# A two-layer decoder on one core: the shared expert's products made to give way and wait for the last routing, and the grouped attention's norm taken per half block

## The chip, the cores and the metric

One Trainium2 chip, one core. The metric is the device time of one execution in microseconds (us). The kernel is written by hand, with one queue of instructions per engine: TensorE (PE, its weight loads PEld), VectorE (DVE), ScalarE (ACT), GpSimd (POOL) and SyncE (SP), which issues most DMAs. Each engine takes its instructions strictly in order.

## What is computed

The input `x` is 64 sequences of 64 tokens with 256 features (4096 tokens), all in float32. Two layers follow each other, each with three sublayers on a layer norm of `x`, whose results are added to `x`:

```python
x = x + _L0_attn_ref(_layernorm(x), ...)    # state-space scan (SSD)
x = x + _L0_xattn_ref(_layernorm(x), ctx)   # latent cross attention
x = x + _L0_ffn_ref(_layernorm(x), ...)     # 7 routed experts (top 2) + 1 shared expert
x = x + _L1_attn_ref(_layernorm(x), ...)    # WKV recurrence
x = x + _L1_xattn_ref(_layernorm(x), ctx, ctx)  # grouped attention, 32 query and 8 key heads
x = x + _L1_ffn_ref(_layernorm(x), ...)     # top 8 of 64, mixed in 8 groups
```

Two of them matter here. In the feed-forward of layer 0 every token goes through a shared expert (up, gate with SiLU, down: three 256x256 products) and through two of seven routed experts of the same form; which two is decided by a small product, a top-2 and a softmax. In the cross attention of layer 1 the normalised `x` is the query, scaled per token by `1/sqrt(var)` and shifted by the mean.

## The kernel before

**Units.** A tile is 128 tokens (32 of them), a half block 2 tiles (16), a block 4 tiles (8). `x` stays in SBUF for the whole run.

**Stages.** `layer0` (L1682) runs the scan and the latent attention of all half blocks and `moe_front` of the blocks 0 to 6. `moe_phase` (L1087) then runs `moe_front` of block 7, `moe_tables` and 38 expert tiles (`moe_tile`, L993). `layer1` (L1664) runs all of layer 1.

**What sets the order.** Each piece of work is a Python generator, called a stream. At build time `Plan` keeps a rough model of when each engine is free and each tile is written. `Plan.play` (L204) always continues the stream that by this model could begin first (`Plan.begin`, L197; ties go by rank), and issues its next piece, up to the next `yield`. A `yield` can name marks that other streams must have set, a number of free PSUM banks, or `ROOM`, which puts the stream in the last rank (1000 and above). What the planner issues is then the fixed order of every engine's queue; the chip does not reorder it.

**The last routing.** `moe_front` (L792) normalises one block, transposes it (`hT_ps`, `mr_hT`), writes it to DRAM (`moe_hT`, from which the shared expert reads), multiplies it with the router's weights (`lT_ps`), transposes the logits (`pl`), and picks two experts per token on DVE (`mr_gate` to `moe_oh`). A product `rk` counts the tokens ahead of each one, DVE works out the slots, and POOL scatters the rows to their experts' slots with 8 indirect DMAs (`moe_hs`). `moe_tables` (L905) then counts the rows of each expert (`cnt`) and works out on DVE which expert each of the 38 tiles belongs to (`mt_int`). SP reads that table before it can load the first tile (`ht`), which PE then transposes (`ht_ps`).

**The shared expert.** `shared(n)` (L1069) does half block n of 16. It loads `sh_hT` (two buffers), and makes three groups of four 128x256 products, `u_ps`, `g_ps` and `d_ps`, with ACT and DVE steps between them (`expert`, L1032), and adds to `x`. Each of these products is asked for with `ROOM`. The half blocks 0 to 7 are also fillers of `moe_phase`: they may begin at once, and one that has not begun when the first expert tile has is left for `layer1`, which runs all that are in `shared_left`.

**Layer 1.** Per half block: `collect` (L1649) adds the experts' rows to `x` with indirect DMAs on POOL, after the shared expert's half block; `wkv_front` and `wkv_scan` (L1145, L1205) end in `wk_po`; two streams `gqa_tile` (L1336) do the grouped attention of one tile each; then comes the feed-forward: `ffn_front` (L1456) for a group of 2 or 4 tiles, `ffn_half`, `ffn_gate` and `ffn_down` (products `gu_ps` and `acc`). The first `ffn_front` also waits for every half block in `shared_left`.

**A tile of the grouped attention.** `gqa_tile` waits for the keys, for the scan of its half block, for the tile two before it and for the feed-forward of the tile nine before it. It takes the norm of its one tile (`norm`, L287: statistics and two small steps on DVE, a power on POOL), writes the query in groups with four `tensor_scalar` of 64 columns on POOL (`gqa_q`), transposes it (`pq`), and goes on to `sc`, a maximum on DVE, `pq` again, `st`, an exponential on ACT (`pT`), `pv`, a copy of `pv` to `oT` on DVE, and `po`.

All engine instructions go through one helper, so all have line L62 in the profile; they are told apart by the tiles that they write and read.

Of the kernel before, what the change touches and what calls it, by code (L numbers as in the profile page):

```python
# [66 lines left out]
class Plan:  # L67
# [5 lines left out]


    ROOM, SOON, LAST = "room", "soon", 1000
    COST = dict(vector=(100, 1.17), scalar=(250, 0.75), gpsimd=(300, 1.75), sync=(380, 0))
    AFTER = dict(tensor=250, vector=150, scalar=150, gpsimd=200, sync=100)

# [118 lines left out]
    def begin(self, item):  # L197

        at, rank, count, stream, n = item
        if n:  # L200
            at = max(at, self.banks[n - 1][0])
        return max(at, self.free.get(self.first_at.get(self.place(stream)), 0.0)), rank, count

    def play(self, streams, fillers=()):  # L204

# [34 lines left out]
class Net:  # L240
# [551 lines left out]
    def moe_front(self, wk, w, b):  # L792

        nc, te, v, gp = self.nc, self.nc.tensor, self.nc.vector, self.nc.gpsimd

        def t(n, s, bufs=1):
            return wk.tile(s, F32, tag="mr_" + n, bufs=bufs, name="mr_" + n)

        yield self.after(("route", b - 1), *(("att", n, t) for n in (2 * b, 2 * b + 1) for t in range(2)))
        f = {}  # L800
        yield from self.norm(wk, b * NT, NT, "mn", f)
        rs, nm = f["rs"], f["nm"]
        ha = w["h"][b % 2]
        for i in range(NT):
            nc.scalar.activation(ha[0][:, i, 0:D], self.x[:, b * NT + i], AF.Identity, bias=nm[:, i:i + 1], scale=rs[:, i:i + 1])
        yield
        hT = wk.tile([P, 2, TB], F32, tag="mr_hT", bufs=1, name="mr_hT")
        for c in range(2):
            yield [1]
            ps = self.mm([P, TB], "hT_ps")  # L810
            for i in range(NT):
                te.transpose(ps[:, i * P:(i + 1) * P], ha[0][:, i, c * P:(c + 1) * P], self.ident)
            yield
            (v.tensor_copy if c else nc.scalar.copy)(hT[:, c], ps)
            self.give(ps)
        yield
        self.load(self.hTd[b], hT)
        self.plan.mark("rows", b)
        nc.scalar.copy(ha[1][:, :, 0:D], ha[0][:, :, 0:D])

        yield [1]
        pq = self.mm([P, P], "lT_ps")
        for c in range(2):
            for i in range(NT):
                te.matmul(pq[32 * i:32 * i + 32], w["r"][:, c], hT[:, c, i * P:(i + 1) * P], start=c == 0, stop=c == 1)
        yield
        lT = t("lT", [P, P])
        nc.scalar.copy(lT, pq)
        self.give(pq)
        yield [1]  # L830
        pl = self.mm([P, NT, 32], "pl")
        te.transpose(pl.rearrange("p n e -> p (n e)"), lT, self.ident)
        yield
        gate, bg, eq, s1 = t("gate", [P, NT, 7]), t("bg", [P, NT, 7]), t("eq", [P, NT, 7]), t("s1", [P, NT])
        oh = w["oh"][:, b]
        v.tensor_add(gate, pl[:, :, 0:7], bc(w["br"], 1, NT))
        self.give(pl)
        v.tensor_add(bg, gate, bc(w["gb"], 1, NT))

        for k in range(2):  # L840
            v.tensor_reduce(s1, bg, AX.X, ALU.max)
            v.tensor_tensor(eq, bg, bc(s1, 2, 7), ALU.is_equal)
            v.tensor_mul(eq, eq, bc(w["rank"], 1, NT))
            v.tensor_reduce(s1, eq, AX.X, ALU.max)
            v.tensor_tensor(oh[:, k], eq, bc(s1, 2, 7), ALU.is_equal)
            if k == 0:
                v.scalar_tensor_tensor(bg, oh[:, 0], -3e38, bg, ALU.mult, ALU.add)
        yield

        both, run = t("both", [P, NT, 7]), w["run"][b % 2]  # L850
        v.tensor_add(both, oh[:, 0], oh[:, 1])
        v.tensor_copy(run[:, 0], w["total"])
        for i in range(NT):
            v.tensor_add(run[:, i + 1], run[:, i], both[:, i])
        w["total"] = run[:, NT]
        yield

        sel, g2, mx, s2 = t("sel", [P, 2, NT, 7]), t("g2", [P, 2, NT]), t("mx", [P, NT]), t("s2", [P, NT])
        v.tensor_mul(sel, oh, bc(gate, 1, 2))
        v.tensor_reduce(g2, sel, AX.X, ALU.add)  # L860
        v.tensor_tensor(mx, g2[:, 0], g2[:, 1], ALU.max)
        v.tensor_sub(g2, g2, bc(mx, 1, 2))
        yield
        nc.scalar.activation(g2, g2, AF.Exp)
        yield
        yield [1]
        rk = self.mm([P, NT, 7], "rk")
        te.matmul(rk, w["before"], both, start=True, stop=False)
        te.matmul(rk, w["ones"], run[:, 0:NT], start=False, stop=True)
        yield  # L870
        slot = t("slot", [P, NT, 7])
        v.tensor_add(slot, rk, bc(w["slot"], 1, NT))
        self.give(rk)
        v.tensor_mul(sel, oh, bc(slot, 1, 2))
        at = w["at"][:, b]
        v.tensor_reduce(at, sel, AX.X, ALU.add)
        v.tensor_copy(w["slots"][:, b], at)
        v.tensor_add(s2, g2[:, 0], g2[:, 1])
        v.reciprocal(s2, s2)
        for k in range(2):  # L880
            v.tensor_mul(ha[k][:, :, D:D + 1].rearrange("p n o -> p (n o)"), g2[:, k], s2)
        yield [("zeros", 0), ("zeros", 1)]
        for k in range(2):
            for i in range(NT):
                yield [Plan.SOON]
                self.moe_row(w, w["slots"][:, b, k, i:i + 1], ha[k][:, i])
        self.plan.mark("route", b)
# [181 lines left out]
    def shared(self, n, fills=False):  # L1069

        if fills:
            yield [Plan.ROOM] + ([("made", MAXT - 4)] if n >= 8 else [])
            if ("begun", 0) in self.plan.marks and n < 8:
                return
            self.shared_left.remove(n)
        wk = self.mid
        yield self.after(("rows", n // 2), ("shared", n - 2))
        b = wk.tile([P, 2, 2, HT], F32, tag="hT", bufs=2, name="sh_hT")
        hT, uT = b[:, 0], b[:, 1]
        self.load(hT, self.hTd[n // 2][:, :, (n % 2) * HT:(n % 2 + 1) * HT])  # L1080
        yield [Plan.ROOM, 1]
        ps = yield from self.expert(wk, None, hT, 4, True, *self.shared_mats, uT, "aT")
        self.nc.vector.tensor_add(self.x[:, 2 * n:2 * n + 2], self.x[:, 2 * n:2 * n + 2], ps)
        self.give(ps)
        self.plan.mark("shared", n)
# [238 lines left out]
    def gqa_turned(self, wk, qa, tag):  # L1324
# [8 lines left out]
        yield [4]  # L1333
        return qT

    def gqa_tile(self, wk, w, n, f):  # L1336
        nc, te, v, gp = self.nc, self.nc.tensor, self.nc.vector, self.nc.gpsimd
        t = n % NT
        yield self.after(("keys", n // NT), ("scan", n // 2), ("gqa", n - 2), ("ffn", n - GQA_LEAD))
        r_ = {}  # L1340
        yield from self.norm(wk, n, 1, "gn", r_)
        qa = w["q"][n % len(w["q"])]
        gp.memset(qa.rearrange("p g k c -> p (g k) c")[:, :, 16:18], 0.0)
        xg = self.x[:, n].rearrange("p (k j g d) -> p g k j d", k=4, j=2, g=4)
        for g in range(4):
            gp.tensor_scalar(qa[:, g, :, 0:16].rearrange("p k (j d) -> p k j d", j=2), xg[:, g], r_["rs"], r_["nm"], ALU.mult, ALU.add)
        qT = yield from self.gqa_turned(wk, qa, "qT")

        sc = [self.mm([P, 4, 2, S], "sc") for _ in range(4)]
# [26 lines left out]
                          start=True, stop=True)  # L1376
        yield
        oT = wk.tile([P, 4, P], F32, tag="oT", bufs=2, name="oT")
        v.tensor_copy(oT, pv.rearrange("p g j s -> p g (j s)"))
        self.give(pv)  # L1380
        yield [1]
        po = self.mm([P, 4, 8, 16], "po")
# [281 lines left out]
    def layer1(self, wk, w_wkv, w_gqa, w_ffn):  # L1664
        self.wkv_padded(wk, w_wkv)
        streams = [(0, self.shared(n)) for n in self.shared_left] + [(1, x) for x in [self.load_ffn(w_ffn), self.prep_ffn(wk, w_ffn)]]
        fs = [{} for _ in range(NH + NBLK)]
        streams += [(n, self.collect(n)) for n in range(NH)]
        for n in range(NH):
            streams += [(n, self.wkv_front(wk, w_wkv, n, fs[n])), (n, self.wkv_scan(wk, w_wkv, n, fs[n]))]  # L1670
        for b in range(NBLK):
            g = fs[NH + b]
            streams.append((2 * b, self.gqa_front(wk, w_gqa, b, g)))
            streams += [(2 * b + t // 2, self.gqa_tile(wk, w_gqa, NT * b + t, g)) for t in range(NT)]
        for i, (n0, nt) in enumerate(self.GROUPS):
            f = {}
            streams.append((n0 // 2, self.ffn_front(wk, w_ffn, i, n0, nt, f)))
            streams += [(h, self.ffn_half(wk, w_ffn, i, h, f)) for h in range(n0 // 2, (n0 + nt) // 2)]
        with self.tc.manual_schedule():
            self.plan.play(streams)  # L1680
# [113 lines left out]
```

## Time and profile before

| what | us |
|---|---|
| median of 3 runs | 2126.09 (2123.85 to 2131.75) |
| the profiled execution | 2121.44 |
| its span, from first to last instruction | 2119.7 |
| busy in the span: PE, DVE, POOL, ACT | 1933.7 (91%), 1343.7 (63%), 845.6 (40%), 791.1 (37%) |

The profiled execution lies 4.65 below the median and 1.74 above its own span. By the timeline `layer0` ends near 823, the first expert tile is transposed at 887, the last product of the expert tiles starts at 1094, the first WKV transpose (`wk_hT`) of layer 1 stands at 1118.9, and the first `gu_ps` at 1251.5. Times in what follows are from the start of the span. In lists of the timeline a line is: start, duration, engine, line, operation, tile written and tiles read, shapes, number of instructions, and in brackets the engine's idle time before it and what ended it. A float32 product of the program is two MATMUL instructions in the trace.

### The profile page before, as it was taken

The numbers are of one execution on the slowest core, as the hardware profiler recorded it, in microseconds if no ns is written. First come the engines' busy times: TensorE is split into PE (matmuls) and PEld (weight loads), VectorE is DVE, ScalarE is ACT, GpSimd is POOL, SyncE is SP. The second block draws the span as 40 slices with busy tenths as digits, with TensorE's granted clock in tenths as the row PEclk, the third lists the DMA queues.
The fourth block names the chain that finished last, engine by engine and source line by source line (L and its number), as shares of the span: only waits on it lengthen the run. The fifth ranks groups of instructions, "written<-read, shape, count | busy, mean of one in ns | idle before, by whom it ended". The sixth has DMA issues, their size and how long they took to land. (4 is left out here: it accounts for less than half of the span.)

```text
span 2119.7 us, 36371 instructions
## 1 busy us (share of the span) xinstructions
PE 1933.7 (91%) x13735; PEld 1548.6 (73%) x13735; DVE 1343.7 (63%) x3149; ACT 791.1 (37%) x1439; POOL 845.6 (40%) x1045
## 2 busy tenths in 40 slices
PE   7989898898989897899988879989899999999998
PEld 6768677687778775688876557767677777777777
DVE  5667776767676773343336887877778676755331
ACT  3425343434334332244433423433334334243220
POOL 2332434343534423111126856667456334432211
PEclk9989999999899998999998879989999999999999
DMA  7963200000000001388844212121111101010010
GB/s 206 348 202 118 67 16 22 16 22 16 22 26 26 22 31 67 132 302 281 276 159 91 29 21 35 15 35 22 22 20 24 19 14 18 9 23 15 17 23 11
DMA packets 167807, 150.43 MB, mean 71 GB/s; under 512 B 76153, under 2 KB 155408, under 8 KB 167632
## 3 DMA queue, kind: packets, MB, share of 16 engines
q1 hardware_dynamic: 152464, 121.61, 19.6%
q0 software_dynamic: 15168, 26.50, 5.1%
q8 instruction: 109, 1.79, 0.3%
q14 instruction: 66, 0.54, 0.1%
HBM read 88.01 MB, written 60.04 MB: 70 GB/s over the span
## 5 line engine op out<-in xcount | busy, mean ns | idle before, releaser
L62 PE MATMUL gu_ps<-hT,ffn_gu 128*128 128x256 f32 x1408 | 337.0, 386 | 5.0 <-DVE gqa_q L62 4.1
L62 PEld LDWEIGHTS gu_ps<-hT,ffn_gu 128*128 128x128 f32 x1408 | 260.2, 192 | 50.4 <-issue 8.4
L62 PE MATMUL acc<-ffn_d,aT 128*128 128x256 f32 x704 | 166.0, 389 | 9.2 <-DVE aT L62 9.2
L62 POOL TENSOR_TENSOR aT<-aT,ffn_sc 128x512 f32<-128x512 f32 (+1 forms) x48 | 69.1, 1440 | 229.1 <-DVE aT L62 197.1
L62 PEld LDWEIGHTS acc<-ffn_d,aT 128*128 128x128 f32 x704 | 134.4, 194 | 34.3 <-DVE aT L62 10.7
L62 PE MATMUL proj<-sf_hT,w_in 128*128 128x256 f32 x640 | 148.2, 389 | 0.0
L62 ACT ACT_TABLE_LOAD x104 | 133.4, 1283 | 21.4 <-PE st L62 7.9
L62 PEld LDWEIGHTS proj<-sf_hT,w_in 128*128 128x128 f32 x640 | 121.7, 194 | 18.5 <-issue 1.8
L62 PE MATMUL po<-xa_vo,ctxT 128*128 128x256 f32 x512 | 121.8, 394 | 4.9 <-ACT ctxT L62 2.8
L62 ACT ACTIVATE aT<-gu_ps 128x512 f32<-128x512 f32 x96 | 48.7, 559 | 203.4 <-PE gu_ps L62 203.3
L62 DVE TENSOR_TENSOR aT<-aT,gu_ps 128x512 f32<-128x512 f32 x96 | 56.9, 633 | 106.2 <-ACT aT L62 106.2
L62 PE MATMUL q_ps<-xn_hT,xa_q 128*128 128x256 f32 x512 | 118.3, 386 | 2.5 <-DVE ctxT L62 1.3
L62 PEld LDWEIGHTS po<-xa_vo,ctxT 128*128 128x128 f32 x512 | 99.4, 198 | 23.1 <-ACT ctxT L62 7.8
L62 POOL DMA_INDIRECT x_sb<-moe_ys,left x64 | 106.6, 1665 | 23.3 <-issue 12.0
L62 PEld LDWEIGHTS q_ps<-xn_hT,xa_q 128*128 128x128 f32 x512 | 96.3, 192 | 22.0 <-ACT xn_hT L62 2.7
L62 POOL DMA_DIRECT2D moe_ys<-y x38 | 26.3, 692 | 207.0 <-ACT y L62 194.4
L62 DVE TENSOR_REDUCE gqa_q<-sc 128x8 f32<-128x512 f32 x128 | 79.3, 681 | 35.4 <-PE sc L62 35.4
L62 DVE TENSOR_TENSOR x_sb<-x_sb,po 128x256 f32<-128x256 f32 x64 | 26.5, 415 | 107.5 <-PE po L62 107.4
L62 DVE SCALAR_TENSOR_TENSOR sf_acc<-proj,ssm_vec,sf_acc 128x252 f32<-128x252 f32 (+2 forms) x192 | 87.3, 472 | 7.5 <-ACT sf_acc L62 3.0
L62 POOL TENSOR_TENSOR p<-p,sm 128x1024 f32<-128x1024 f32 x32 | 60.8, 1907 | 73.0 <-DVE sm L62 42.5
L62 POOL DMA_INDIRECT moe_hs<-moe_h,moe_slots x64 | 64.4, 1006 | 56.9 <-ACT gT L62 27.1
L62 ACT COPY qT<-pq 128x512 f32<-128x512 f32 x64 | 37.4, 586 | 115.2 <-PE pq L62 115.2
(367 smaller groups left out, 4338.7 us busy)
## 6 DMA issues: line engine op xcount, KB each, us to landing
moe_hs<-moe_zero SPq DMA_DIRECT2D x30, 1088.0 KB
pack<-in_moe_pack_dram SPq DMA_DIRECT2D x38, 770.0 KB
ht<-moe_hs SPq DMA_DIRECT2D x32, 272.0 KB
moe_ys<-y POOLq DMA_DIRECT2D x32, 256.0 KB, 5.7
bias<-moe_bias SPq DMA_DIRECT2D x38, 128.0 KB
x_sb<-in_x_dram SPq DMA_DIRECT2D x8, 512.0 KB
moe_hT<-mr_hT SPq DMA_DIRECT2D x8, 512.0 KB
sh_hT<-moe_hT SPq DMA_DIRECT2D x16, 256.0 KB
```

The source lines that it names most:

```text
L62: return do(*a, **k)
```

## The change

It has five parts, all in the order of work but for two.

```diff
+    POLITE = 1500
@@ Plan.begin
-        return max(at, self.free.get(self.first_at.get(self.place(stream)), 0.0)), rank, count
+        at = max(at, self.free.get(self.first_at.get(self.place(stream)), 0.0))
+        return at + (self.POLITE if stream.__name__ == "shared" and rank >= self.LAST else 0), rank, count
@@ moe_front, behind the transpose of the logits
+        self.plan.mark("logits", b)
@@ shared
         if fills:
-            yield [Plan.ROOM] + ([("made", MAXT - 4)] if n >= 8 else [])
+            yield [Plan.ROOM, ("logits", NBLK - 1)]
@@ layer 1's attention
+    def gqa_norm(self, wk, h, f):
+
+        yield self.after(("scan", h), ("gqa", 2 * h - 3))
+        r = f["norm", h] = {}
+        yield from self.norm(wk, 2 * h, 2, "gn", r)
+        self.plan.mark("normed", h)
+
     def gqa_tile(self, wk, w, n, f):
-        yield self.after(("keys", n // NT), ("scan", n // 2), ("gqa", n - 2), ("ffn", n - GQA_LEAD))
-        r_ = {}
-        yield from self.norm(wk, n, 1, "gn", r_)
+        yield self.after(("keys", n // NT), ("normed", n // 2), ("gqa", n - 2), ("ffn", n - GQA_LEAD))
+        rs, nm = (f["norm", n // 2][k][:, n % 2:n % 2 + 1] for k in ("rs", "nm"))
-        for g in range(4):
-            gp.tensor_scalar(qa[:, g, :, 0:16].rearrange("p k (j d) -> p k j d", j=2), xg[:, g], r_["rs"], r_["nm"], ALU.mult, ALU.add)
+        for j in range(2):
+            gp.tensor_scalar(qa[:, :, :, 8 * j:8 * j + 8], xg[:, :, :, j], rs, nm, ALU.mult, ALU.add)
-        v.tensor_copy(oT, pv.rearrange("p g j s -> p g (j s)"))
+        nc.scalar.copy(oT, pv.rearrange("p g j s -> p g (j s)"))
@@ layer1
+            streams += [(h, self.gqa_norm(wk, h, g)) for h in (2 * b, 2 * b + 1)]
```

- A shared expert's product counts as 1500 ns later than it could begin when the planner picks what comes next, in `moe_phase` and in `layer1`.
- The fillers of `moe_phase` may begin only when the logits of the last block have been transposed.
- The norm of the grouped attention becomes a stream of its own, for two tiles at once.
- The query of a tile is written with two `tensor_scalar` of 128 columns instead of four of 64.
- The copy `oT` moves from DVE to ACT.

## The prediction

> **What bounds the kernel now.** First the page's busy times and slices: they say which engine to count on, and where it does not work.
>
> ```profile
> PE 1933.7 (91%) x13735; PEld 1548.6 (73%) x13735; DVE 1343.7 (63%) x3149; ACT 791.1 (37%) x1439; POOL 845.6 (40%) x1045
> ...
> PE   7989898898989897899988879989899999999998
> ...
> PEclk9989999999899998999998879989999999999999
> ```
>
> PE is the bound nearly everywhere, so work that only moves costs the same wherever PE has it. What can change is PE's idle and slow time. The slices show two holes: around slice 15, where layer 0 turns into expert tiles, and slices 20 to 23, the start of layer 1. So next the busy time of stretches whose ends I took from PE's timeline (columns: length, then busy PE, PEld, DVE, ACT, POOL with instruction counts, granted PE clock, DMA share, GB/s).
>
> ```profile
> 823.40:887.40 64.00, 50.51 (x224) 41.06 (x224) 25.72 (x91) 21.01 (x43) 13.06 (x25) 0.92 0.24 80
> 1095.60:1118.90 23.30, 13.17 (x62) 10.69 (x60) 6.49 (x17) 5.50 (x13) 10.77 (x13) 0.85 0.63 184
> 1118.90:1208.00 89.10, 76.36 (x545) 57.59 (x545) 68.51 (x119) 36.53 (x67) 71.15 (x66) 0.92 0.29 49
> 1208.00:1251.50 43.50, 31.17 (x230) 21.10 (x225) 32.61 (x64) 13.77 (x30) 23.34 (x25) 0.69 0.22 28
> 1373.00:1404.20 31.20, 19.58 (x229) 13.80 (x228) 28.64 (x66) 11.59 (x22) 19.96 (x23) 0.78 0.20 38
> 1404.20:2119.70 715.50, 684.01 (x5424) 540.85 (x5422) 432.88 (x856) 246.34 (x405) 284.25 (x327) 0.99 0.10 18
> ```
>
> From 1404 on PE is busy 684 of 715 us at clock 0.99: little to win. The other rows hold the change. Last, PE's and POOL's timeline of the first hole.
>
> ```profile
> 829.52 6.54 PE L62 MATMUL u_ps<-sh_hT,sh_w 128*128 128x256 f32 x16 [6.18 <-DMA sh_hT<-moe_hT]
> 835.90 0.60 PE L62 MATMUL hT_ps<-ident,moe_h 128*128 128x128 f32 x4
> ...
> 842.71 0.64 PE L62 MATMUL lT_ps<-mr_hT,moe_r 128*32 128x128 f32 x16
> ...
> 845.12 0.27 PE L62 MATMUL pl<-ident,mr_lT 128*128 128x128 f32 x1
> ...
> 848.68 3.62 PE L62 MATMUL g_ps<-sh_hT,sh_w 128*128 128x256 f32 x16
> 852.14 0.30 PE L62 MATMUL rk<-mr_both,moe_before 128*128 128x28 f32 x2
> ...
> 875.20 0.28 PE L62 MATMUL cnt<-moe_run,moe_ones 128*128 128x7 f32 x2
> ...
> 887.39 0.63 PE L62 MATMUL ht_ps<-ident,ht 128*128 128x128 f32 x4 [0.66 <-DMA ht<-moe_hs]
> ```
>
> The routing's short products stand in PE's queue behind the shared expert's long ones, and everything up to `ht_ps` hangs on them. `moe_h` is ready at 829.7; `hT_ps` starts at 835.9.
>
> **Part 1: the last routing, −10.** In the changed kernel's order both `hT_ps`, `lT_ps` and `pl` stand ahead of every shared product. From 829.7 I count: 8 transposes on a slow clock 2.1 (four took 1.39 after the idle time at 1118.9), two copies side by side 0.7 with hand-over 0.2, 16 `lT_ps` about 1.2, copy and `pl` 0.9: `mr_gate` near 835.1 instead of 845.9. DVE needs 3.9 from there to the end of `moe_run` (849.85), so 839.0. One `u_ps` group stands ahead of `rk`, and its load now follows the write of `moe_hT` in SP's queue: from a load's issue at 840.8 to its product at 845.2 were 4.4, an upper end. With that `rk` comes at 841, without it at 839; before, 852.1. The scatter comes as much earlier. Then the order has 10 groups of shared products between `rk` and `cnt` and 6 between `cnt` and `ht_ps` (before: 9 and 5). A group is 1.73 when PE runs on; between 852.5 and 886.7 14 groups took 34.2, so 2.44. At 2.44, 16 groups put `ht_ps` at 841 + 39 = 880, that is −7; at 1.9 at 871, −16. The chain from `cnt` to `ht_ps` (12.2) fits beside 6 groups at 2.0. I take −10, ends −5 and −16.
>
> **Part 2: what it leaves for later, +3.** Eight half blocks of the shared expert were finished in this hole; now five and two thirds are. Seven groups, 12.1 us, go behind the expert tiles. There lies cover: after its last product there (1093.77) PE waited for `x` (expert rows written, collected, normed) with 9.3 us idle ahead of `wk_hT` at 1118.9, 25.1 in all. The new order has 13 groups in that stretch where 7 were. At 2.0 each (six groups from 1095.60 to 1107.58) that is 26: cover, and 1 late. At 2.44 it is 31.7, 6.6 late. SP's loads for them are the same 16, in the same queue. I take +3; without the cover it is +12.
>
> The hole also left a slow clock: four transposes took 1.39 at 1118.9 and 0.60 at 1145.9. Likewise the first 16 `u_ps` took 6.54 after 6.18 of waiting, 3.62 later, so a cold start costs 2.9 here. Either kernel has one in part 1; part 2 loses one, which I leave as margin. The Trainium skill, "TensorE: Matmul & The Clock Gate", section "Why this matters for your kernels", speaks against part 1: it asks for no idle gaps over about 3 us between bursts, and clearing PE for the routing makes such a gap. By that rule the sum would be up to 2.9 worse, since the routing's products and the first shared ones would all run slowly; the trace agrees that PE is slow there, but it was before too, so I add nothing.
>
> **Part 3: the start of layer 1, +6.** `ffn_front` waits for the last shared half block. Before, its first transposes stood ahead of the third pair of attention tiles (1208.0, 89.1 after the first `wk_hT`). Now the last `d_ps` stands behind the fourth attention tile and `ffn_front` behind the third `wk_po` (before at 1242.5) and the fourth `wk_hT`. Against that, the first WKV products no longer wait for four shared groups between them (5 us), and with `gu_ps` not queued behind the fourth WKV its routing takes 25.6 (1208.0 to `smT_ps` 1233.6) and not 43.5. So the first `gu_ps` comes 115 + 25.6 + 8 = 149 after the first `wk_hT`, not 132.6. Work up to it, counted at the rates at which PE runs on (0.43 a 128x256 product, 0.11 a transpose, 1.08 for 8 `st`), is 97 instead of 90, so 7 of the 16 are paid in, and a few us of the rest come back in the colder stretch: +6, ends −8 and +27.
>
> **Part 4: the second stall, −12.** From 1373.0 to 1404.2 PE held some 12 us of work at those rates; it waited for a feed-forward front that came too late.
>
> ```profile
> 1377.52 4.54 PE L62 MATMUL acc<-ffn_d,aT 128*128 128x256 f32 x12 [4.08 <-DVE aT L62]
> ...
> 1388.31 1.22 PE L62 MATMUL pq<-ident,gqa_q 128*128 128x128 f32 x3 [4.04 <-POOL gqa_q L62]
> ```
>
> Between that front's transposes and the first `gu_ps` after it stood 21 us of PE work; in the new order 38, as the attention now runs ahead of the feed-forward. The front needs about 35 (1364.6 to 1400). The loss was 19. But DVE, at 28.6 of 31.2 there, has the same work to do: −12, ends −19 and 0.
>
> **Part 5: attention's norm and copies, −4.** Per tile POOL had four `gqa_q` at a median of 0.39, and 0.55 for `fr_h` of 256 columns: by interpolation 128 columns take 0.45, so 0.9 instead of 1.6. DVE loses 32 `oT` of 0.69 (22 us) and 32 small steps of 0.16; ACT gains 32 copies at 0.59 (its `qT`), beside its 37% load, and two table loads of 1.28. Waits of PE that name these are few: `pq` for POOL 11.8 in all (11 of it in single waits at 1203, 1260, 1388 and 1520; the third lies in part 4's stall), `po` for `oT` 3.9. The copy now stands behind ACT's exponentials, which its queue could make late. −4, ends −12 and +6.
>
> **Sum.** −10 + 3 + 6 − 12 − 4 = −17. The profiled execution took 2121.4, so 2104.4; it lies 4.65 below the median, to which runs will be compared: **2109**.
>
> **Rivals.** *Given back:* parts 1 and 2 cancel (−10 + 12) and parts 4 and 5 bring as little as part 3 costs: 2126 + 2 − 3 = 2125. For it: the work is the same and PE is 91% busy. Against it: the 9.3 us hole. *Slower:* the late `ffn_front`. If the first `gu_ps` comes a whole half block later (31 us, the step from the third `wk_hT` at 1186.0 to the fourth at 1217.0) with only 4 of work paid in, part 3 costs 27, and parts 4 and 5 win nothing in the same in-order queues: −10 + 3 + 27 = +20, 2146. It decides once the front costs over 7 more than it pays in. For it: PE at clock 0.69 from 1208 on, with no other work to take; against it: the faster first WKV steps. *More:* all parts near their good ends, which the 47 us of idle time and the slow clock from 1095.6 to 1251.5 and at 1373 allow: −15 and +1 for the first two, −1 and −16 for the next, −7 for the last, −38 in all, 2088.
>
> **How the numbers follow.** Forecast (2098 to 2118) 0.5, given back 0.2, slower 0.18, more 0.12. A measurement tells 0.5% from no change: 2115.5 to 2136.7 is the same. The forecast is faster in 0.44 and the same in 0.06; "more" is faster; "given back" is the same but for 0.01 each way; that makes faster 0.57, same 0.24, slower 0.19. The range 2085 to 2140 leaves out the worse part of "slower" and the better half of "more".
>
> **What would show it.** Right: `ht_ps` by 880, `wk_hT` near 1112 with PE working up to it, first `gu_ps` near 1261 (1112 + 149), and no stall of 20 us behind the second feed-forward group. Wrong: shared groups at over 2.5 us before `wk_hT`, the first `gu_ps` after 1275, or PE waits on ACT `oT`.

## The result, and the profile after

The changed kernel took 2090.74 us in the median (2088.72 to 2094.99) against 2126.56 for the kernel before on the same chip: a ratio of 0.9837, with a 95% interval of 0.9813 to 0.9861. That is 36 us of medians. The profiled executions, 2121.44 and 2091.92, lie 29.5 apart; the traces can explain only these 29.5, since the one lies below its median and the other above.

The page after, first the engines' busy times, then PE's slices and clock:

```profile
PE 1920.3 (92%) x13735; PEld 1538.2 (74%) x13735; DVE 1312.9 (63%) x3085; ACT 812.3 (39%) x1473; POOL 822.2 (39%) x965
...
PE   7989898899899897899998879989999999999998
...
PEclk9999899999899998899999979999999999999999
```

PE runs the same 13735 instructions in 13.4 us less of busy time (the mean granted clock is 0.967, before 0.959), and the span is 29.6 shorter, so PE is also idle 16.2 less. A slice of 52 us is too coarse for the rest: counted from 0 as in the prediction, busy time rises from 8 to 9 in slices 20 and 28 and the clock from 8 to 9 in slices 21, 22 and 26, while the clock's 7 in slice 23 stays.

The same stages as before, with ends moved. Two starts are not the same instruction: the second row starts with the last expert product (before, just behind it), and the third ahead of the first feed-forward front, whose transposes now stand at 1224.97 (before at 1208.0). (Columns: length, then busy PE, PEld, DVE, ACT, POOL with instruction counts, granted PE clock, DMA share, GB/s.)

```profile
823.40:877.00 53.60, 40.46 (x174) 31.05 (x173) 21.80 (x85) 15.01 (x33) 12.57 (x25) 0.87 0.26 86
1082.99:1116.60 33.61, 26.81 (x118) 21.13 (x117) 9.22 (x21) 9.93 (x23) 11.17 (x13) 1.00 0.59 138
...
1206.00:1258.40 52.40, 38.43 (x325) 26.85 (x325) 45.55 (x91) 22.06 (x44) 37.01 (x36) 0.80 0.19 30
...
1342.50:1381.50 39.00, 36.11 (x412) 27.27 (x410) 32.78 (x71) 17.59 (x32) 19.34 (x23) 1.00 0.02 4
1381.50:1411.00 29.50, 25.81 (x227) 19.66 (x227) 23.86 (x47) 14.14 (x25) 21.27 (x20) 1.00 0.42 61
1411.00:2090.00 679.00, 649.97 (x5122) 516.99 (x5120) 393.51 (x762) 245.02 (x401) 254.80 (x254) 0.99 0.10 18
```

Three rows matter. The stretch ahead of the first `wk_hT` now has PE busy for 26.81 of 33.61 at clock 1.00, where it was 13.17 of 23.30 at 0.85: the hole is filled, but from the end of the last expert product (1084.82) the stretch is 31.8 us long, 8.5 longer. The second stall is gone. From 1342.5 to 1381.5 the front of feed-forward group 2 (tiles 4 to 7) runs, for which PE had waited there: 36.11 of 39.00 at clock 1.00. Behind it PE has 25.81 of 29.50. The same front took 1364.6 to 1400 before, with 24.31 of 35.40 at 0.81:

```profile
1364.60:1400.00 35.40, 24.31 (x241) 17.90 (x240) 28.69 (x70) 15.05 (x26) 17.27 (x21) 0.81 0.12 24
```

The start of layer 1 (1206 to 1258) still has PE idle for a quarter of the time, at clock 0.80.

What PE does beside that front, by its timeline (start, duration, operation, shapes):

```profile
1342.54 0.60 PE L62 MATMUL hT_ps<-ident,fr_h 128*128 128x128 f32 x3
...
1350.13 3.72 PE L62 MATMUL acc<-ffn_d,aT 128*128 128x256 f32 x16
...
1355.73 0.38 PE L62 MATMUL pl<-ident,fr_lT 128*128 128x128 f32 x2
...
1358.91 1.99 PE L62 MATMUL gu_ps<-hT,ffn_gu 128*128 128x256 f32 x8
1360.74 3.62 PE L62 MATMUL acc<-ffn_d,aT 128*128 128x256 f32 x16
1364.19 0.60 PE L62 MATMUL weT_ps<-ident,fr_sc 128*64 128x128 f32 x4
...
1367.41 1.99 PE L62 MATMUL gu_ps<-hT,ffn_gu 128*128 128x256 f32 x8
...
1375.63 0.28 PE L62 MATMUL scaT_ps<-ident,fr_sca 128*32 128x128 f32 x1
...
1380.87 0.66 PE L62 MATMUL smT_ps<-ident,fr_soft 128*128 128x128 f32 x4
```

The front's own steps are `hT_ps`, `pl`, `weT_ps`, `scaT_ps` and `smT_ps`. Between them stand `gu_ps` and `acc` of the groups ahead, 11 us in the lines shown, and in the lines left out some 16 us of attention and WKV products; no wait of PE in the stretch is over 1.43.

The first hole, PE's timeline of the changed kernel:

```profile
829.53 2.80 PE L62 MATMUL hT_ps<-ident,moe_h 128*128 128x128 f32 x8 [4.98 <-ACT moe_h L62]
...
834.16 0.47 PE L62 MATMUL pl<-ident,mr_lT 128*128 128x128 f32 x1 [0.39 <-ACT mr_lT L62]
837.28 3.75 PE L62 MATMUL u_ps<-sh_hT,sh_w 128*128 128x256 f32 x8 [2.65 <-DMA sh_hT<-moe_hT]
840.83 0.46 PE L62 MATMUL rk<-mr_both,moe_before 128*128 128x28 f32 x2
```

```profile
862.95 0.28 PE L62 MATMUL cnt<-moe_run,moe_ones 128*128 128x7 f32 x2
...
876.89 0.66 PE L62 MATMUL ht_ps<-ident,ht 128*128 128x128 f32 x4 [0.47 <-DMA ht<-moe_hs]
```

The routing stands first now: `rk` at 840.83 instead of 852.14, `ht_ps` at 876.89 instead of 887.39.

What the put-off products cost, PE's timeline ahead of the first `wk_hT` (1116.57; before 1118.9):

```profile
1094.38 1.99 PE L62 MATMUL g_ps<-sh_hT,sh_w 128*128 128x256 f32 x8 [0.56 <-ACT sh_hT L62]
1098.03 1.99 PE L62 MATMUL d_ps<-sh_w,gT 128*128 128x256 f32 x8 [1.65 <-DVE gT L62]
1099.86 1.89 PE L62 MATMUL u_ps<-sh_hT,sh_w 128*128 128x256 f32 x8
...
1116.57 0.69 PE L62 MATMUL wk_hT<-ident,wk_h 128*128 128x128 f32 x4
```

In most half blocks PE waits 1.65 for DVE's `gT` and 0.56 for ACT's `sh_hT`, with two buffers and hardly any other products to put between. From 1084.82 to 1116.57 are 13 groups in 31.75 us, 2.44 each. So the 10.8 us by which the last expert tile finished earlier (its last product starts at 1082.99, not 1093.77) shrink to 2.3 at `wk_hT`.

**Counted work.** Clock times mislead here, because the kernels do the same work in another order. So I rate every product at what it takes when PE runs on (0.433 us a 128x256 product, 0.109 a transpose, and so on; 1716 us in all, the same for every variant) and read from each trace when the same amount is left to do. It is a working of mine, good to a few us. The change from before to after, in us, minus for gained, by what is left: +2.8 down to 1040 left (routing done, fewer shared products done), −3.0 from there to 840 (just behind the first `wk_hT`), +0.2 to 800, −7.1 to 660, −12.0 to 600 (the second stall) and −10.4 to the end: −29.5. Next to nothing has been won up to the start of layer 1: 2.3 at the first `wk_hT`, where both kernels have done 31 of the 48 groups of the shared expert, and 0.0 with 800 left.

### The profile page after: what moved, and what is told of

Same layout as the page of the kernel before. It is cut to its first block, busy times and chain, and to the rows that moved or that the text cites. A ratio compares the mean times of both kernels' runs of the same rounds, so it can differ in the third digit from the quotient of the medians.

```text
span 2090.1 us, 36286 instructions
## 1 busy us (share of the span) xinstructions
PE 1920.3 (92%) x13735; PEld 1538.2 (74%) x13735; DVE 1312.9 (63%) x3085; ACT 812.3 (39%) x1473; POOL 822.2 (39%) x965
## 4 chain that ended last, share of the span: by engine, by line
PE 70%; DVE 17%; POOL 5%; ACT 3%; issue 3%; DMA 1%; SPq 1%; DVEq 0%; POOLq 0%; ACTq 0%
PE gu_ps L62 14%; PE po L62 7%; PE acc L62 6%; PE q_ps L62 5%; PE proj L62 5%; PE u_ps L62 4%; PE g_ps L62 3%; PE d_ps L62 3%; PE sc L62 3%; PE pv L62 2%; PE wk_po L62 1%; PE st L62 1%; POOL x_sb L62 1%; PE pq L62 1%; DVE sf_acc L62 1%
## 5 line engine op out<-in xcount | busy, mean ns | idle before, releaser
L62 PE MATMUL gu_ps<-hT,ffn_gu 128*128 128x256 f32 x1408 | 332.0, 383 | 4.0 <-ACT pT L62 3.8
L62 POOL DMA_DIRECT2D moe_ys<-y x38 | 26.3, 692 | 207.6 <-ACT y L62 195.1
```

The costliest lines, as they stand in the source:

```text
L62: return do(*a, **k)
```

## The experiments

Three theories. **1**: the reasons of the prediction; the parts have separate worths that add up, most of it from the order of the shared expert and the routing. **2**: attention's cheaper operations (POOL's `gqa_q`, `oT` off DVE) bring most of it. **3**: what counts is the order of PE's whole queue in layer 1, which any edit of the planner's input redraws; the parts need not add up. All runs are compared with the kernel before on the same chip.

**Parts alone.** `routing_only` is the kernel before with the giving way and the wait for the logits:

```diff
...
+        return at + (self.POLITE if stream.__name__ == "shared" and rank >= self.LAST else 0), rank, count
...
+        self.plan.mark("logits", b)
...
+            yield [Plan.ROOM, ("logits", NBLK - 1)]
```

> Edit: the kernel before with the routing half of the change alone (shared products 1.5 us later in the planner's eyes, fillers from the last logits on); attention as before. Theory 1 (the gain is PE's: the routing goes first, its cost is covered ahead of the first wk_hT, and giving way lets attention run ahead of the feed-forward, so that the second feed-forward group's front comes in time): the first ht_ps near 877, in the order 41 us of PE work between that front and its first gu_ps (before 19, changed kernel 38), so no second stall; about 20 of the 36 us gained, 2106 (2100 to 2112). Theory 2 (the attention edits are the main gain, by a lighter DVE): 2118 or more. Theory 3 (the order is a lottery, any reshuffle moves the time by 10 or more either way): no forecast, and the parts do not add up.

Measured: 2122.34, ratio 0.9978 (0.9966 to 0.9990). Only 4 us; theory 1 wanted 20. What PE waited for from 1205 to 1275 (us in total, times, longest), first here, then in the changed kernel:

```profile
PE hT_ps L62 <- POOL fr_h L62: 5.7, 2, 5.3
PE pk L62 <- DVE wk_mix L62: 5.5, 1, 5.5
PE d_ps L62 <- DVE gT L62: 5.3, 1, 5.3
PE wk_po L62 <- POOL wk_o L62: 5.1, 1, 5.1
```

```profile
PE sc L62 <- DVE gqa_q L62: 3.2, 1, 3.2
PE d_ps L62 <- DVE gT L62: 2.9, 1, 2.9
```

Four waits of over 5 us stand in the one, none over 3.2 in the other, though the shared expert gives way in both.

`attention_only` is the kernel before with the norm by half block, two wide `gqa_q` and `oT` on ACT.

> Edit: the kernel before with the attention half alone (norm per half block, two wide gqa_q, oT on ACT); the shared expert as before. Theory 1: ht_ps stays near 887, the order holds only 23 us of PE work between the second group's front and its first gu_ps, so a stall of 10 to 19 us stays near 1375 to 1405; gain 4 to 10, 2117 to 2123. Theory 2: gain 20 or more, 2106 or less. Theory 3: no forecast, the two halves' gains do not add up to 36.

Measured: 2138.88, ratio 1.0062 (1.0040 to 1.0084): slower by 13 us. Theories 1 and 2 both miss. The operations are cheaper and the kernel slower, so their cost alone does not decide. Where it is lost, by its stretches, and the wait that cost PE most there (us in total, times, longest):

```profile
1370.00:1402.00 32.00, 22.28 (x144) 15.45 (x144) 29.15 (x50) 10.89 (x18) 25.39 (x27) 0.73 0.17 27
1402.00:1432.00 30.00, 22.91 (x262) 15.71 (x261) 27.61 (x56) 13.97 (x27) 13.95 (x17) 0.89 0.16 34
```

```profile
PE wk_hT L62 <- ACT wk_h L62: 6.8, 3, 3.9
```

PE is busy 45 of 62 us, where before was busy 50 of the same 62: the second stall is not gone but longer, and by counted work it takes 97 us instead of 82 (the table below).

`no_giving_way` is the changed kernel without the first part:

```diff
-    POLITE = 1500
+    POLITE = 0
```

> Edit: the changed kernel with the 1.5 us set to 0; the wait for the logits and the attention edits stay. Theory 1: ht_ps near 878 as in the changed kernel, but the work put off is only covered (net 0 to 3), and the stall behind the second group's front stays (23 us of PE work ahead of it, as in attention alone): 2113 to 2121. If part 1 were worth its 10 us in full: 2106 or less. Theory 2: within 8 us of the changed kernel, 2099 or less.

Measured: 2135.55, ratio 1.0046 (1.0031 to 1.0061). Theories 1 and 2 both miss here too.

`no_logits_wait` is the changed kernel with its fillers free to begin at once:

```diff
-            yield [Plan.ROOM, ("logits", NBLK - 1)]
+            yield [Plan.ROOM]
```

> Edit: the changed kernel with fillers that may begin at once, as before; they still count as 1.5 us later. Theory 1: the routing is held up again by at most the shared products that are under way, ht_ps within 4 us of 887, but what is done early need not be done later: within 6 us of the changed kernel, 2088 to 2097. If the wait for the logits were what gains: 2101 or more.

Measured: 2121.28, ratio 0.9980 (0.9966 to 0.9993), where theory 1 had 2088 to 2097. Taking away either the giving way or the wait takes away nearly all of the gain or more, while the two alone bring 4 us. The worths do not add: −4 and +13 apart, −36 together. Theory 1's claim of a sum falls.

**Order against operations.** Here the planner is told of one kernel's operations, so that PE's queue stays instruction for instruction, while the other kernel's are issued. Only `gqa_q` and `oT` are swapped; the norm per half block goes with the order. The copy, as an example (`gqa_q` likewise):

```diff
+        self.plan.enter("scalar", "copy", (oT, pv.rearrange("p g j s -> p g (j s)")), {})
+        v.real.tensor_copy(oT, pv.rearrange("p g j s -> p g (j s)"))
-        nc.scalar.copy(oT, pv.rearrange("p g j s -> p g (j s)"))
```

> Changed kernel with its PE queue kept instruction for instruction, and the planner told of the new operations, but the old ones issued in attention: the oT copies on VectorE instead of ScalarE, and four narrow gqa_q operations on GpSimd instead of two wide ones. Theory 3 (the order of PE's queue in layer 1 is what is worth the time, the operations little): 2088 to 2100 us, the second stretch 1380 to 1411 still nearly full of PE work. Theory 2 (the freed GpSimd and VectorE time is needed for the gain): 2105 us or more, with po waiting on VectorE oT and st on gqa_q.

> Kernel before with its PE queue kept instruction for instruction, and the planner told of the old operations, but the new ones issued in attention (oT copies on ScalarE, two wide gqa_q operations; the norm stays by block). Theory 3: 2118 to 2130 us, the second stall stays, since PE's queue still has the same 19 us of work between the second group's front and its first gu_ps. Theory 2: 2116 us or less.

In each pair the traces show PE's 13735 instructions in the same order. Measured: old operations in the new order 2101.49, ratio 0.9888 (0.9857 to 0.9919); new operations in the old order 2126.00, ratio 1.0014 (0.9997 to 1.0031). So the new operations are worth nothing in the old order (the interval is 1 us won to 7 lost) and about 11 in the new one (0.9888 less 0.9837, of 2124; some 3 to 19 with both intervals); the order is worth 24 without them. Theory 3 holds in the main; its 2088 to 2100 was missed by little.

**Is it a lucky order?** A change of one constant of the planner, with no purpose, redraws the order and touches no operation:

```diff
-    COST = dict(vector=(100, 1.17), ...)
+    COST = dict(vector=(103, 1.17), ...)
```

Theory 3 splits here: in 3a the place of one piece of work decides, that front of group 2; in 3b the order is a mere draw.

> Kernel before, with one cost constant of the planner (a VectorE operation, 100 to 103 ns) changed for no purpose: no instruction is added, removed or moved to another engine, only the order of the queues changes in layer 1 (618 lines of PE's listing differ). PE's queue has 18 us of work between the second group's front and its first gu_ps, against 19 before. Theory 3a (the place of the second group's front decides): 2118 to 2134 us. Theory 3b (the order is a draw: any change of it moves the time by tens of us either way): outside that, anywhere from 2095 to 2150.

> Changed kernel with the same purposeless edit (cost of a VectorE operation 100 to 103 ns): the change stays whole, its order in layer 1 is drawn anew (670 lines of PE's listing differ). PE's queue has 45 us of work between the second group's front and its first gu_ps, against 38 in the changed kernel. Theory 3a: 2084 to 2100 us. Theory 3b: over 2100, with the second stall or another one of its size back in layer 1.

Measured: 2134.25, ratio 1.0047 (1.0028 to 1.0066), and 2121.98, ratio 0.9977 (0.9957 to 0.9997). The first is at 3a's upper end, the second 22 above it. But the edit had also redrawn layer 0 (PE's queue differs from its 92nd row on): by counted work both are some 20 us late already at the end of layer 0, ahead of everything that the change touches, and 23 with 1040 left. The pair differs by 12 us. So I repeated the edit from the start of layer 1 on:

```diff
+        self.plan.COST = dict(Plan.COST, vector=(103, 1.17))
         self.wkv_padded(wk, w_wkv)
```

> Kernel before, the purposeless edit (cost of a VectorE operation 100 to 103 ns in the planner) from the start of layer 1 on, so that all ahead of it stays as it was, unlike in null_before; PE's queue is that of before up to its 694th row. It has 18 us of work between group 2's front and its first gu_ps. Theory 3a: the second stall stays (16 us or so between 660 and 640 us of PE work to go), 2112 to 2130 us. Theory 3b: no bound, 2095 to 2150.

> Changed kernel, the same purposeless edit from the start of layer 1 on; PE's queue is the changed one up to its 730th row (near 1230 us), with 45 us of work between group 2's front and its first gu_ps. Theory 3a: no second stall, so 16 us or more of the gain stay: 2085 to 2108 us. Theory 3b: over 2108 us.

Measured: 2116.98, ratio 0.9954 (0.9937 to 0.9971), and 2103.54, ratio 0.9898 (0.9872 to 0.9924): 13 us apart. Both lie within 3a's ranges; 3b's lower bound of 2108 for the second fell. The stretch from the first transpose of group 2's front to its `smT_ps`, first in `null_layer1_before`, then in `null_layer1_after`:

```profile
1377.50:1406.50 29.00, 18.28 (x193) 13.44 (x191) 22.97 (x62) 7.21 (x15) 16.98 (x21) 0.65 0.19 33
```

```profile
1328.00:1377.50 49.50, 44.22 (x395) 33.59 (x394) 40.14 (x76) 22.07 (x37) 24.39 (x21) 0.97 0.10 17
```

PE is busy 18.28 of 29.00 at clock 0.65 in the one, 44.22 of 49.50 at 0.97 in the other: the stall stays and goes as 3a said. All the same, the useless edit made the kernel before 7 us faster and the changed one 13 slower: 3b has its share.

**The front of group 2, moved by itself.** `late_front_after` leaves the changed queue as it is up to its 789th row and then holds that front back:

```diff
+        at += 5000 if stream.__name__ == "ffn_front" and stream.gi_frame.f_locals["n0"] == 4 else 0
```

> Changed kernel with the front of group 2 (tiles 4 to 7) made to give way by 5000 ns in the planner: PE's queue is the changed one up to its 789th row, and then has 4 us of work between that front and its first gu_ps, against 38. Theory 3a: the second stall is back, whole: 2106 to 2125 us, the difference from the changed kernel all behind 1345 us. Theory 3b: within 10 us of the changed kernel, 2081 to 2101.

Measured: 2141.30, ratio 1.0072 (1.0048 to 1.0096): 50 us above the changed kernel, over 3a's range and far outside 3b's. By counted work it is within 4 us of the changed kernel until 1359 us, and loses 54 in the next 60 us of work. Stretches of its trace, then PE's timeline inside them:

```profile
1380.00:1429.00 49.00, 37.73 (x361) 25.53 (x360) 36.97 (x74) 21.33 (x40) 27.89 (x30) 0.87 0.14 16
1429.00:1475.00 46.00, 24.00 (x150) 13.65 (x150) 26.46 (x56) 8.82 (x18) 15.09 (x17) 0.51 0.03 6
```

```profile
1449.92 2.94 PE L62 MATMUL hT_ps<-ident,fr_h 128*128 128x128 f32 x8 [1.52 <-POOL fr_h L62]
...
1455.30 0.69 PE L62 MATMUL pl<-ident,fr_lT 128*128 128x128 f32 x2 [0.53 <-ACT fr_lT L62]
1461.04 1.03 PE L62 MATMUL weT_ps<-ident,fr_sc 128*64 128x128 f32 x4 [5.05 <-DVE fr_sc L62]
...
1465.77 0.37 PE L62 MATMUL scaT_ps<-ident,fr_sca 128*32 128x128 f32 x1 [1.06 <-DVE fr_sca L62]
1469.43 1.09 PE L62 MATMUL smT_ps<-ident,fr_soft 128*128 128x128 f32 x4 [3.29 <-DVE fr_soft L62]
...
1476.48 2.55 PE L62 MATMUL gu_ps<-hT,ffn_gu 128*128 128x256 f32 x8
```

From 1449.92 the front's products stand alone in PE's queue: to 1475.00 PE is busy 10.92 of 25.10 us, at clock 0.50, with waits of 5.05 and 3.29 for DVE and nothing left to put between. The attention and WKV products ahead of them, from 1429, fill only 13.08 of 20.90, at 0.52. A front without cover stalls PE, as part 4 of the prediction had it.

`hold_before` is the opposite move. It holds back the products of group 2 in the kernel before, so that more work lies behind the front:

```diff
+        return at + (2000 if stream.__name__ == "ffn_half" and stream.gi_frame.f_locals["h"] == 2 else 0), rank, count
```

> Kernel before with one addition to its planner: the steps of the feed-forward half that opens group 2 (tiles 4 and 5) give way by 2000 ns to products that are ready. Nothing of the change is in it; PE's queue is that of before up to its 818th row (near 1370 us), and has then 32 us of work between the front of group 2 and its first gu_ps, against 19 before and 38 changed. Theory 3a (that cover decides the second stall, 15 to 18 us in every run so far): 2108 to 2114 us, nothing different ahead of 1370. Theory 3b (the order is a draw, the cover beside the point): 2118 us or more.

Measured: 2140.96, ratio 1.0076 (1.0050 to 1.0102): slower by 17, where 3a forecast 10 to 16 faster. A clear miss. Its stretches, and what PE waited for from 1378 to 1480 (us in total, times, longest):

```profile
1378.00:1410.00 32.00, 20.08 (x235) 13.74 (x231) 29.69 (x68) 12.22 (x24) 20.38 (x22) 0.84 0.20 40
1410.00:1450.00 40.00, 33.06 (x307) 23.36 (x308) 31.73 (x55) 14.32 (x27) 29.48 (x32) 0.87 0.24 30
```

```profile
PE pq L62 <- POOL gqa_q L62: 4.9, 3, 4.0
PE acc L62 <- DVE aT L62: 4.5, 2, 4.1
PE po L62 <- DVE oT L62: 4.0, 3, 2.9
```

The stall is as before (20.08 of 32), and then goes on: 33.06 of 40 at clock 0.87, on attention's and WKV's short products, which wait for POOL and DVE themselves; DVE is busy 29.69 of 32.

But this run does not test the cover that it was made to test. PE's order is that of before not up to 1370 but up to 1404.22, where before starts the first `gu_ps` of group 2. The front's last product, `smT_ps`, stands ahead of that. First before, then `hold_before`:

```profile
1393.84 1.06 PE L62 MATMUL smT_ps<-ident,fr_soft 128*128 128x128 f32 x4
...
1404.22 1.89 PE L62 MATMUL gu_ps<-hT,ffn_gu 128*128 128x256 f32 x8
```

```profile
1399.21 0.86 PE L62 MATMUL smT_ps<-ident,fr_soft 128*128 128x128 f32 x4
...
1411.38 1.99 PE L62 MATMUL wk_po<-wkv_o,wk_o 128*128 128x256 f32 x8 [1.49 <-POOL wk_o L62]
```

So between the front's first product and its last both kernels have the same 15 us of work, and PE loses the same 15 us there. The 13 us that the edit added (32 against 19) stand behind the front, ahead of the `gu_ps` of group 2. So the 17 us are the price of putting attention and WKV products ahead of these, and say nothing of the cover. The forecasts had the wrong measure: work up to the first `gu_ps` after the front is not all cover for the front. Up to `smT_ps` the changed kernel has 34 us, not 38.

For all 14 kernels, the table gives the counted work in us from the front's first product to its last, the front's own 4 included (inside), and how many of the 66 `gu_ps` products of group 1 the program has still to issue when it issues the first transpose of group 2's front (left). The other columns are the times in us for the counted work from 800 to 660 us to go, from 660 to 600 (stall) and from 600 to the end:

| kernel | inside | left | 800 to 660 | stall | 600 to 0 |
|---|---|---|---|---|---|
| after | 34 | 18 | 187.9 | 69.7 | 661.4 |
| new_order_old_ops | 34 | 18 | 186.9 | 76.0 | 663.2 |
| null_after | 39 | 54 | 193.4 | 67.2 | 670.7 |
| null_layer1_after | 39 | 54 | 195.1 | 67.2 | 670.2 |
| routing_only | 40 | 34 | 202.1 | 76.6 | 667.8 |
| no_logits_wait | 44 | 38 | 200.6 | 74.5 | 659.1 |
| before | 15 | 8 | 195.0 | 81.7 | 671.8 |
| old_order_new_ops | 15 | 8 | 188.4 | 87.8 | 672.3 |
| hold_before | 15 | 8 | 195.9 | 100.8 | 669.3 |
| null_before | 11 | 0 | 194.5 | 85.2 | 659.7 |
| null_layer1_before | 11 | 0 | 196.7 | 85.2 | 659.4 |
| attention_only | 19 | 0 | 195.8 | 97.3 | 669.6 |
| no_giving_way | 19 | 0 | 194.9 | 97.2 | 669.8 |
| late_front_after | 4 | 0 | 189.9 | 123.7 | 655.0 |

With 34 us or more inside and 18 or more left, PE loses 5 to 12 us between the front's first product and its last (the time less the counted work), and the stall column is 67 to 77. With 19 or less inside and 8 or fewer left, it loses 14 to 18, and the column is 82 to 124. (In all six kernels of the upper part 10 to 33 us of the front lie in the column before.) Two reasons fit: there is more work inside the front, or more of it is ready, such as the `gu_ps` of the group ahead. No run tells them apart. A hint for the second is `attention_only`: the 15 us inside its front besides the front's own are all attention and WKV, and PE lost 15 us there, as it did in before with 11. Both lines were drawn after the runs; the forecasts went by the work up to the first `gu_ps`. Nor is a covered front a gain by itself: over the two columns 800 to 660 and stall together `routing_only` takes 279 us and `no_logits_wait` 275, against 277 before.

The table also says what the giving way does: the six kernels of the upper part have it (the seventh with it is `late_front_after`, whose front I moved). In these the first `ffn_front` comes with 758 to 764 us of work left, in the kernels without it with 774 to 777; the feed-forward starts later against attention, and its products are still there when the next front needs cover.

The outer columns do not sort that way: they spread over 15 and 17 us, with no tie to the change that I found. I put that down to the draw.

## Why the prediction was right or wrong

- **Direction and range right, size half.** −17 was forecast, −36 measured, the time that the prediction gave to "more", though not by that rival's way (all parts near their good ends). Under the two redrawn orders the same change gave −12 and −13, a little short of the forecast; of the 36 some 23 belong to this one pair of orders. No run shows that another edit would keep it.
- **Part 1, −10: right in time, worth nothing.** `rk` came at 840.83 (forecast 841), `ht_ps` at 876.89 (880); of the terms, the 8 `hT_ps` rated at 2.1 took 2.80. By counted work the kernel was then 2.8 behind, since seven groups had been left for later. The rule weighed against this part in the Trainium skill ("TensorE: Matmul & The Clock Gate", "Why this matters for your kernels": no idle gaps over some 3 us) agrees with the trace as far as it goes: after waits of 4.98 and 2.65 the first 8 instructions of `u_ps` took 3.75, later ones 1.89. It changed nothing, since before had such a start as well (6.54 for its first 16, after a wait of 6.18).
- **Part 2, +3: mis-sized.** From the last expert product to `wk_hT` 8.5 us were given back. I had rated 13 groups at 2.0, 26 us against 25.1 of cover; they took 2.44, the figure that I had measured in the first hole and set aside for the upper end. A group ran no faster at clock 1.00, since it was the waits for `gT` and `sh_hT` that paced it. At 2.44 the sum has 6.6; the other 1.8 is the last expert product itself, which stands in the 25.1 and which I left out. Parts 1 and 2 together were forecast at −7 and gave −2.3 at `wk_hT`, −0.2 just behind it.
- **Part 3, +6: wrong sign.** The first `gu_ps` came at 1258.36 (forecast 1261, from 149 behind `wk_hT`; it was 142). But with 740 us of work left, just behind it, the changed kernel was 6.7 ahead. I had it 16 later than before, with 7 of that paid in by other work; it was 9 later, and by counted work about 8 were paid in. And just behind its first `gu_ps` the kernel before waited 3.16 for POOL's `gqa_q`, at 1259.99, where the changed kernel runs on, which I had not counted.
- **Part 4, −12: right,** −12.0 by counted work, and −18 against the redrawn kernel before in both draws (85.2 to 67.2). The reason given, 38 us of work behind the front instead of 21, was counted to the first `gu_ps`; inside the front it is 34 instead of 15. That fits all 14 kernels, and so do the ready `gu_ps`; both were found in hindsight, and which of them decides stays open. `hold_before` missed because its added work stood behind the front.
- **Part 5, −4: not one number.** 0 in the old order, about −11 in the new. The operations cost what I took, by their groups in the changed kernel (count, then duration in ns: least, median, most; first and last start):

```profile
L62 POOL TENSOR_SCALAR gqa_q<-x_sb,gn_rs,gn_nm x64: 437/448/1970, 1154.1 to 1942.5; 128x128 f32<-128x128 f32 x64
```

```profile
L62 ACT COPY oT<-pv x32: 562/585/620, 1173.3 to 1972.9; 128x512 f32<-128x512 f32 x32
```

Two wide `gqa_q` take 0.90 (forecast 0.9), a copy 0.59 (0.59), and PE waited for it 1.2 us in all. What a freed engine is worth depends on what PE has queued behind it. In `attention_only`, with no products of group 1 left at the second front, the same operations went with a loss of 13; which of its edits redrew the order so was not tried.
- **The sum itself** was the step that failed. It took five parts as separate. They share one in-order queue that is written anew for every edit: the giving way and the wait without attention's part brought 4 us, attention's without these cost 13. (In the sum of the rival "given back" the −3 has no source; no number here rests on it.)

Left open: whether the amount of work inside the front or its readiness decides; why the stretch from 800 to 660 took 202 us in `routing_only` and 188 in the changed kernel, and whether the half-block norm is the cause; and the spread of the last 600 us of work. None of the runs beat the changed kernel.

## What to carry to other kernels

Where a planner at build time writes each engine's whole queue, draw the order anew a few times with edits that mean nothing, on both sides, before a gain of 1% is put down to a change: here such edits moved the same kernel by 7 and 13 us. To hide a long chain of short products, count the work that the queue has between the chain's first product and its last: 13 us that stood behind the last one covered nothing here, and cost 17. And compare two orders where the same work is left, since a product that comes earlier on the clock may only have left its work for later.

## What the runs showed that was not expected

A wait costs more than its length: in `late_front_after` PE's granted clock fell to 0.51 over 46 us in which it was about half busy, and 8 `hT_ps` took 2.94 there, where 4 take 0.60 in the changed kernel. And making two operations cheaper without touching PE's order (`old_order_new_ops`) won 6.6 us in one stretch (195.0 to 188.4) and lost 6.1 in the next (81.7 to 87.8).
